# 64 more no-ops a step on TensorE, two behind each W1 product: a step of 768 instruction places

## The chip, the core and the metric

The kernel runs on one core of a Trainium2 chip. A core has five engines with an instruction stream each: TensorE (PE in the profile; its weight loads are shown apart, as PEld), VectorE (DVE), ScalarE (ACT), GpSimd (POOL) and SyncE (SP), which here issues nearly all DMAs. They run side by side and wait for each other through semaphores. The metric is the device time of one launch in microseconds, the median of several executions.

## The reference

A block of a transformer with cross attention, over 128 sequences of 128 tokens, model width 256, 16 heads of 16, hidden width 1024, all in float32:

```python
q = (query @ Wq + bq).reshape(b, s, N_HEADS, D_K).transpose(0, 2, 1, 3)
k = (key @ Wk + bk)...          # v in the same way
scores = jnp.einsum('bhqd,bhkd->bhqk', q, k) / jnp.sqrt(jnp.float32(D_K))
scores = jnp.where(j < i + mask, scores, NEG_INF)      # mask is 0
attn = jax.nn.softmax(scores, axis=-1)                 # row 0 is set to zero
ctx = jnp.einsum('bhqk,bhkd->bhqd', attn, v)
x = layer_norm(query + ctx @ Wo + bo, ln1_g, ln1_b)
ffn = jax.nn.relu(x @ W1 + b1) @ W2 + b2
out = layer_norm(x + ffn, ln2_g, ln2_b)
```

## The kernel before

The sequences are taken in 64 pairs, and the work on a pair is spread over several turns of a software pipeline. `steps(9, 60)` (L1669) emits 52 turns of it, here called steps or slots; slots 7 and 8 and the last ones are written out by hand, op by op, in other orders. The order inside a step is the list `order` in `step_tables` (L1643). It is an order of emission: each engine runs its own instructions of it strictly in that order, and waits where an operand isn't ready. A name in the list with slot p works on pair p for the scores, on older pairs for the later stages: p - 2 for the context and Wo, p - 3 for the hidden layer, p - 4 for the second layer.

TensorE's part of a step, in its order, is this:

- `scores` (`scores_both`, L494, matmuls at L510): 32 float32 products on strips of 32 rows. A float32 product is two weight loads and two matmuls, so the profile counts 64 matmuls.
- the queries of the next pair (`q261`, `q457`, `q3`; L354), the output projection (`out`, `o457`, `o3`; L722), keys (`k`, L284) and values (`v`, L414), with parts of the following mixed in.
- the hidden layer, class `Hidden`, stages H1 to H7 (matmuls at L1282). Seven block products in place of eight; each stage is a loop over NI = 4, so there are 28 W1 products a step. H1 reads `x1T`, the transposed first norm, which comes back from DRAM by DMA (`x1out` and `x1in`, L1004 to L1012); H1 is the first to wait for it.
- the second layer, class `Second`, stages S1 to S7 (L1184), again 28 products. They accumulate in tiles named pX, py and pz.
- `weigh` (L657 and L667): softmax weights times values, 48 small products, whose 96 matmuls stand straight ahead of the scores of the next step. The last stages ahead of it are, in order, H7, S7, H2, H4, H3.

`empty(n)` (L219) emits n no-ops on TensorE, with `nofuse=True` so that they stay instructions of their own. They compute nothing and nothing waits for them. `Second` spreads `pads` of them over its 28 products, through the difference of two rounded quotients, so that 56 are two behind each:

```python
1188                     self.done += 1
1189                     empty(self.pads * self.done // (7 * K) - self.pads * (self.done - 1) // (7 * K))
```

`Hidden` emits none. `second7` (L1472) and `hidden7` (L1475) make the two objects of a slot, once each, for the slots from 7 to 62; the tail makes its own, without pads.

An instruction place is one instruction of TensorE's stream: a weight load, a matmul, a no-op or a semaphore instruction. A step of the loop has the same places each time.

## Time and profile before

| what | us |
|---|---|
| median of 3 runs | 1508.13 |
| lowest, highest | 1504.8, 1508.3 |
| the profiled execution | 1508.24 |
| its span, from first to last instruction | 1506.3 |
| DMA queue q1 (data) | 218.36 MB, 60.7% of 16 engines' time |
| largest group of matmuls, L1282, x1T times w | 128.9 busy, 960 of 277 ns |
| scores, L510 | 108.4 busy by the page's group, 3840 matmuls in 60 steps |

The page's busy times count an engine as busy while it has an instruction in flight. Matmuls overlap, and their ends are modelled, so TensorE's busy share is high even where it could go faster; an idle time printed for it is a lower bound of what it lost. In a row of the timeline stand the start, the length, the engine, the source line, the operation, the tiles written and read, the shape and the count of merged instructions; in square brackets the idle time before it and what ended it. "issue" says that the engine waited for nothing that the profile shows. In the view by stretch of time the columns are the stretch, its length, busy time (with the count) of PE, PEld, DVE, ACT and POOL, TensorE's granted clock, the DMA engines' share and GB/s.

### The profile page before, as it was taken

To read this page: it belongs to the slowest core of one execution; us is meant where nothing else is said; L and a number is where in the kernel's file an instruction comes from. 1 tells how busy PE (TensorE), PEld (TensorE's weight loads), DVE (VectorE), ACT (ScalarE), POOL (GpSimd) and SP (SyncE) were. 2 spreads that over 40 slices of the span, in tenths; PEclk is the share of its full clock that TensorE was granted. 3 is DMA by queue.
4 is the path that set the end of the run, shared out by engine and by line. 5 is a ranking of instruction groups with operands and counts; after the bars stand their busy time and mean duration, and the time that the engine had idled before them with its cause. 6 is when DMAs were issued, how large, how long until landed. Compare 5 with 4: busy or idle time off the path is not lost.

```text
span 1506.3 us, 58023 instructions
## 1 busy us (share of the span) xinstructions
PE 1472.7 (98%) x20054; PEld 1385.7 (92%) x20054; DVE 1314.4 (87%) x2955; ACT 1334.7 (89%) x5336; POOL 1375.2 (91%) x1772
## 2 busy tenths in 40 slices
PE   9999999999999999999999999999999999999998
PEld 6788899999999999999999999999999999999988
DVE  7999789889889898898898888988888988988876
ACT  5658899999999999999999989999999999999963
POOL 7888799999999999899999999999999998999998
PEclk9999999999999999999999999999999999999999
DMA  8546566666666656666566666666666566664461
GB/s 202 109 95 155 132 152 155 150 157 144 165 154 148 155 145 157 161 144 157 140 154 155 160 145 149 157 144 162 150 156 148 138 164 159 145 152 130 127 178 57
DMA packets 433155, 222.34 MB, mean 148 GB/s; under 512 B 290412, under 2 KB 394092, under 8 KB 432876
## 3 DMA queue, kind: packets, MB, share of 16 engines
q1 hardware_dynamic: 431356, 218.36, 60.7%
q8 instruction: 173, 2.83, 0.8%
q14 instruction: 106, 0.87, 0.2%
q10 hardware_dynamic: 1520, 0.27, 0.1%
HBM read 86.78 MB, written 35.80 MB: 81 GB/s over the span
## 4 chain that ended last, share of the span: by engine, by line
PE 90%; DMA 2%; DVE 2%; SPq 2%; issue 2%; POOL 1%; ACT 1%; ACTq 0%; DVEq 0%; POOLq 0%
PE phs L1282 25%; PE pX L1184 10%; PE py L1184 7%; PE pz L1184 7%; PE pk L284 7%; PE pss L510 6%; PE pv L414 6%; PE pq L354 6%; PE po L722 5%; PE pc L667 4%; PE pc L657 2%; DMA x1T<-x1t 2%; PE ph L1034 1%; SPq L623 1%; DVE sm L524 1%
## 5 line engine op out<-in xcount | busy, mean ns | idle before, releaser
L1114 ACT ACTIVATE sm<-pss,nmx 128x128 f32<-128x128 f32 x944 | 329.9, 376 | 6.1 <-DVE nmx L1097 3.9
L1114 ACT ACTIVATE sm<-sm,nmx 128x64 f32<-128x64 f32 x944 | 320.1, 362 | 0.7
L589 DVE STREAM_TRANSPOSE tb<-sm 128x1024 f32<-128x1024 f32 x186 | 225.8, 1216 | 3.3 <-POOL sm L563 3.2
L1319 ACT ACTIVATE hT<-hT,b1e_c 128x256 f32<-128x256 f32 x480 | 209.4, 499 | 8.2 <-DVE hT L1310 6.4
L1114 ACT ACTIVATION_READ_ACCUMULATOR sm<-pss,nmx 128x1 f32 x912 | 196.6, 216 | 0.0
L1114 ACT ACTIVATION_READ_ACCUMULATOR sm<-sm,nmx 128x1 f32 x912 | 195.5, 214 | 0.0
L1097 DVE TENSOR_REDUCE nmx<-pss 128x4 f32<-128x512 f32 x236 | 161.3, 685 | 2.2
L404 ACT ACTIVATE kT<-pk,bkh,half 128x256 f32<-128x256 f32 x252 | 139.0, 579 | 2.8 <-PE pk L284 2.8
L1282 PE MATMUL phs<-x1T,w 128*128 128x128 f32 x960 | 128.9, 277 | 5.3 <-DMA x1T<-x1t 5.2
L1282 PEld LDWEIGHTS phs<-x1T,w 128*128 128x128 f32 x960 | 120.1, 193 | 12.9 <-issue 10.3
L524 DVE TENSOR_TENSOR sm<-pss,neg 128x256 f32<-128x256 f32 (+1 forms) x276 | 114.6, 436 | 18.5 <-PE pss L510 13.2
L1282 PE MATMUL phs<-xS,w 128*128 128x128 f32 x960 | 127.0, 275 | 0.0
L510 PE MATMUL pss<-kT,qT 32*64 32x256 f32 (+1 forms) x3840 | 108.4, 330 | 15.9 <-issue 15.5
L414 PE MATMUL pv<-wv,cT 128*128 128x256 f32 x512 | 121.4, 380 | 0.0
L284 PE MATMUL pk<-cT,wk 128*128 128x256 f32 x504 | 119.4, 380 | 0.1
L1208 DVE TENSOR_TENSOR t<-t,pX 128x128 f32<-128x128 f32 x180 | 59.0, 328 | 67.6 <-PE pX L1184 67.6
L1282 PE MATMUL phs<-xS,w1t 128*128 128x128 f32 x960 | 117.8, 275 | 0.0
L1282 PEld LDWEIGHTS phs<-xS,w 128*128 128x128 f32 x960 | 116.8, 192 | 0.1
L1282 PEld LDWEIGHTS phs<-xS,w1t 128*128 128x128 f32 x960 | 112.6, 192 | 0.1
L510 PEld LDWEIGHTS pss<-kT,qT 32*64 32x64 f32 x3840 | 83.5, 131 | 31.7 <-issue 23.4
L1091 DVE TENSOR_TENSOR pss<-pss,neg 128x256 f32<-128x256 f32 x236 | 100.1, 425 | 10.2 <-PE pss L510 10.1
L414 PEld LDWEIGHTS pv<-wv,cT 128*128 128x128 f32 x512 | 93.0, 191 | 10.8 <-issue 0.6
(231 smaller groups left out, 4735.2 us busy)
## 6 DMA issues: line engine op xcount, KB each, us to landing
pT<-tb SPq DMA_DIRECT2D x976, 96.0 KB
x1t<-tbx SPq DMA_DIRECT2D x252, 64.0 KB
x1T<-x1t SPq DMA_DIRECT2D x63, 256.0 KB
out_dram<-t SPq DMA_DIRECT2D x63, 256.0 KB
xb<-in_x_dram SPq DMA_DIRECT2D x124, 128.0 KB
cb<-in_ctx_dram SPq DMA_DIRECT2D x124, 128.0 KB
x<-in_x_dram SPq DMA_DIRECT2D x31, 512.0 KB
wt<-rtd SPq DMA_DIRECT2D x29, 256.0 KB
```

What stands on the lines that cost most here:

```text
L284: nc.tensor.matmul(ps[:, m * TP : (m + 1) * TP], w[:, k, m * P : (m + 1) * P], src[:, k, :], start=(k == 0), stop=(k == KC - 1),)
L404: nc.scalar.activation(st["kT"][:, m, e, :], pk[:, m * TP : (m + 1) * TP], AF.Identity, bias=bkh[:, m, e : e + 1], scale=half[:, e : e + 1],)
L414: nc.tensor.matmul(pv[:, s * D : (s + 1) * D], st["cT"][:, k, s * P : (s + 1) * P], wv[:, k, :], start=(k == 0), stop=(k == KC - 1),)
L510: nc.tensor.matmul(st["sps", hi][r][s * HP : (s + 1) * HP, m * 2 * n : (m + 1) * 2 * n].rearrange("p (e j) -> p e j", e=2), st["qT"][strip ...
L524: nc.vector.tensor_tensor(probabilities(p, hi)[:, 4 * r : 4 * r + 4, :], st["sps", hi][r][:, : 4 * n].rearrange("p (n j) -> p n j", j=n), ...
L589: nc.vector.transpose(st["tb"][:, :, at : at + 256].rearrange("p j (n a) -> p n j a", a=32), probabilities(p, hi).rearrange("p h j -> p (h ...
L1091: nc.vector.tensor_tensor(ps[:, :, HP:], ps[:, :, HP:], neg[:, 1, None, :].to_broadcast([P, 4, HP]), ALU.add)
L1097: nc.vector.tensor_reduce(maxima(p, 1)[:, 4 * r : 4 * r + 4], st["sps", 1][r].rearrange("p (n j) -> p n j", j=P), AX.X, ALU.max, negate=True,)
L1114: nc.scalar.activation(sm[:, h, :], src, AF.Exp, bias=nmx[:, h : h + 1], scale=1.0, **({"accum_out": su[:, u : u + 1]} if summed else {}))
L1184: nc.tensor.matmul(out, left(k), right(k), start=(first and k == 0), stop=(k == K - 1), skip_group_check=True,)
L1282: nc.tensor.matmul(ps[:, i * P : (i + 1) * P].rearrange("p (n a) -> p n a", a=32), left(i), right, start=(i == 0 and which not in self.ONT ...
L1319: nc.scalar.activation(self.hT[:, f], self.hT[:, f], AF.Relu, bias=b1e_c[:, f : f + 1], scale=1.0,)
```

## The change

Each W1 product gets two no-ops behind it in the slots from 9 on, and four in slots 7 and 8; the second layer's no-ops go from 56 to 64 a step. That is 56 + 8 = 64 more places a step, of which the change's description says that a step then counts 768, and that the first score product is moved to place 153 of 256. No operand, tile, bank or order of the other instructions is changed.

```diff
-        def __init__(self, p, banks=None, onto=None):
+        def __init__(self, p, banks=None, onto=None, pads=0):
             st = states[p]
+            self.pads = pads
             if banks:
...
                     left(i), right, start=(i == 0 and which not in self.ONTO),
                     stop=True, skip_group_check=True,
                 )
+                empty(self.pads)
...
     def second7(p):
-        return once("second", p - 4, lambda: Second(p - 4, 56, (5, 7, 3)))
+        return once("second", p - 4, lambda: Second(p - 4, 64, (5, 7, 3)))
 
     def hidden7(p):
-        return once("hidden", p - 3, lambda: Hidden(p - 3, {1: 2, 2: 7, 5: 6, 4: 5}, {3: 5, 6: 1, 7: 1}))
+        return once("hidden", p - 3, lambda: Hidden(p - 3, {1: 2, 2: 7, 5: 6, 4: 5}, {3: 5, 6: 1, 7: 1}, 4 if p < 9 else 2))
```

## The prediction

> **What bounds the kernel now.** I read the page first, then the table of waits of TensorE, then TensorE's timeline over the steady loop.

> ```profile
> span 1506.3 us, 58023 instructions
> PE 1472.7 (98%) x20054; PEld 1385.7 (92%) x20054; DVE 1314.4 (87%) x2955; ACT 1334.7 (89%) x5336; POOL 1375.2 (91%) x1772
> ...
> PEclk9999999999999999999999999999999999999999
> ...
> q8 instruction: 173, 2.83, 0.8%
> ...
> PE 90%; DMA 2%; DVE 2%; SPq 2%; issue 2%; POOL 1%; ACT 1%; ACTq 0%; DVEq 0%; POOLq 0%
> ```

> TensorE is the bound: busy for 98% of the span, 90% of the chain that ended last, its clock at nine tenths or more in every slice. What is left to gain on it is 33 us of idle time and whatever the modelled ends of matmuls hide. The q8 line matters below: instructions come in 173 packets that hold 2.83 MB, so 16.4 KB each. TensorE has 20054 matmuls, 20054 weight loads, 3180 no-ops and about a thousand semaphore instructions, some 44,270 in all; 2.83 MB over these is 64 bytes each, and a packet is 256 instructions. So q8 carries TensorE's own instructions, in **blocks of 256 places**.

> Who does TensorE wait for?

> ```profile
> PE pss L510 <- issue: 15.5, 21, 1.0
> PE phs L1282 <- DMA x1T<-x1t: 5.2, 6, 3.5
> ```

> Twenty-one waits, in the score products alone, are on nothing that the profile knows ("issue"). The timeline, cut to the scores (64 matmuls a step), shows where they fall:

> ```profile
> 213.59 1.62 PE L510 MATMUL pss<-kT,qT 32*64 32x128 f32 x64
> ...
> 554.50 1.62 PE L510 MATMUL pss<-kT,qT 32*64 32x128 f32 x64
> 576.81 1.62 PE L510 MATMUL pss<-kT,qT 32*64 32x128 f32 x64
> 599.12 1.11 PE L510 MATMUL pss<-kT,qT 32*64 32x128 f32 x28
> 601.16 1.11 PE L510 MATMUL pss<-kT,qT 32*64 32x256 f32 x36 [0.94 <-issue]
> 622.96 1.57 PE L510 MATMUL pss<-kT,qT 32*64 32x128 f32 x60
> 625.49 0.43 PE L510 MATMUL pss<-kT,qT 32*64 32x128 f32 x4 [0.97 <-issue]
> 646.62 1.62 PE L510 MATMUL pss<-kT,qT 32*64 32x128 f32 x64
> 669.63 1.62 PE L510 MATMUL pss<-kT,qT 32*64 32x128 f32 x64
> 692.12 1.11 PE L510 MATMUL pss<-kT,qT 32*64 32x128 f32 x28
> 693.91 1.11 PE L510 MATMUL pss<-kT,qT 32*64 32x256 f32 x36 [0.69 <-issue]
> ...
> 1381.52 1.62 PE L510 MATMUL pss<-kT,qT 32*64 32x128 f32 x64
> ```

> Two scores run through, one breaks behind 28 matmuls, one behind 60, and so on with period four. A matmul and its load are two places, so the breaks stand 56 and 120 places behind the first score product. From the break at 625.49 to that at 693.91 it is three steps less 64 places; were these block starts, three steps less 64 must be a multiple of 256, and with a step near 700 places only 704 fits (2048, eight blocks). The change's 768 less its 64 gives the same 704. **The break is the start of a block that has not arrived.** The second witness is q8 itself: the view of DMA packets, asked for 690.9 to 692.7 us, shows one packet there, and none from 687.5 to 690.9 or from 692.7 to 694:

> ```profile
> q8 instruction: 1, 0.02, 5.7%
> ```

> So the block whose absence ends at 693.91 was in flight at 691 to 692.7, about 1.3 us before its first instruction ran.

> What a break costs, from the view of busy time by stretch, with the two whole steps without one:

> ```profile
> 554.50:576.81 22.31, 22.31 (x324) 21.49 (x317) 20.25 (x48) 21.36 (x89) 21.36 (x29) 1.00 0.66 154
> 576.81:599.12 22.31, 22.31 (x323) 21.49 (x317) 20.36 (x48) 21.35 (x89) 21.35 (x29) 1.00 0.64 158
> 622.96:625.93 2.97, 2.00 (x71) 1.55 (x65) 1.86 (x5) 2.58 (x6) 2.57 (x4) 1.00 0.35 82
> 669.63:671.25 1.62, 1.62 (x71) 1.42 (x65) 1.56 (x5) 1.48 (x4) 1.29 (x3) 1.00 0.49 118
> 692.12:695.00 2.88, 2.19 (x72) 1.47 (x65) 1.63 (x5) 2.58 (x6) 2.47 (x4) 1.00 0.39 93
> ```

> A clean step is 22.31 us, TensorE busy throughout, ACT and POOL (the fourth and fifth columns of busy time) near 21.36: a floor that holds twice running. Broken scores take 2.97 or 2.88 instead of 1.62: 1.35 for a printed wait of 0.97 (0.38 more), 1.26 for 0.69 (0.57 more). With 13 breaks of the first sort and 8 of the second, the 21 cost 15.5 + 13 x 0.38 + 8 x 0.57 = **25 us**. Check: the 51 step starts from 213.59 to 1381.52 lie 1167.9 us apart, 51 x 22.31 is 1137.8, the excess 30.1; so about 5 us belong to something else, mainly to this:

> ```profile
> 656.15 1.13 PE L1282 MATMUL phs<-x1T,w 128*128 128x128 f32 x8 [0.47 <-DMA x1T<-x1t]
> ```

> **The change, part by part.**

> *Where blocks now begin.* Slot 27 (622.96) has a block start 120 places behind its first score product. Slot 9 is 18 steps earlier, 18 x 704 = 49.5 blocks, so there it stands at 120 + 128 = 248, which is also 8 ahead. Slots 7 and 8 gain 28 x 4 + 8 = 120 no-ops each, 240 before slot 9's scores: 248 - 240 = **8 places behind the first score product**. From then on 704 + 64 = 768 is three blocks, and every step has this. The other two starts are 248 ahead of the scores and 264 behind.

> *Do the breaks go?* Ahead of the scores stand, counting back, the weighing of values (96 matmuls, 192 places, 5 semaphores), H3 and H4 (four products of four places and now eight no-ops each), then H2. 248 places back is the last product of H2. Timings from the timeline of a clean approach:

> ```profile
> 665.38 1.06 PE L1282 MATMUL phs<-x1T,w 128*128 128x128 f32 x8
> 666.27 1.06 PE L1282 MATMUL phs<-x1T,w1t 128*128 128x128 f32 x8
> 667.16 1.06 PE L1282 MATMUL phs<-xS,w 128*128 128x128 f32 x8
> 668.15 0.43 PE L657 MATMUL pc<-pT,vd 128*32 128x64 f32 x16
> ```

> H2 starts at 665.38, H4 at 666.27, so TensorE is at that block start at about 666.1 and eight places into the scores at 669.7: 3.6 us. The sequencer is there earlier. How much, the no-ops tell, which it runs itself; the view by source line, from 682 to 684.25, beside the loads of the same products (second fence):

> ```profile
> L221 PEldq NOP  x24: 13/13/13, 682.1 to 684.2; - x24
> ```

> ```profile
> 683.29 0.97 PEld L1184 LDWEIGHTS pz<-w,hT 128*128 128x128 f32 x8
> 684.19 0.97 PEld L1184 LDWEIGHTS py<-w,hS 128*128 128x128 f32 x8
> 685.08 0.97 PEld L1184 LDWEIGHTS pz<-wt,hT 128*128 128x128 f32 x8
> ```

> These 24 no-ops belong to the three products; the first is done 1.3 us and the last 1.8 us before their loads. I take 1.5, so 5.1 us pass between the sequencer's entry into a block and the need for the next. What a block needs is bounded by the broken steps: at 692.12 the previous start is 200 places ahead of the scores, in H3's last product, 1.8 us before them in the clean approach: TensorE is there at 690.3, the sequencer at 688.8, and the next block ran at 693.91, 5.1 us later. At 622.96 it lies 136 ahead, inside the weighing, whose 192 places take 1.48 us and where the sequencer is hardly ahead: about 621.6, and 625.49 is 3.9 later. Need 3.9 to 5.1, given 5.1: no break, or one of a few tenths. I put 0.1 us a step, **+5**, between 0 and 20 (0.4 a step). The block entered 8 places behind has some 9 us until the next start, behind H1; the third likewise.

> *The added no-ops.* Two behind each W1 product, 56, and 8 more behind W2 products (64 over 28, two or three each). Their price on the sequencer lies between the 13 ns of the row and (684.2 - 682.1) / 24 = 88 ns, which includes the product's own places; so 0.8 to 5.6 us a step. A product padded twice takes the sequencer about 0.17 us, TensorE 0.89 / 4 = 0.22. TensorE hides them, **0**, while the sequencer is ahead. Without that cover, each costs up to 0.09. With four no-ops (slots 7 and 8) a product needs up to 0.35 and outruns its cover of 1.5 us: 56 products lose at most 0.13 each, 7 us; much of slot 7 waits for data anyway, so I take **+1.3**.

> *What is late next.* H1's wait for x1T. In steps without a break it costs about 5 us over 29, 0.17 each; broken scores give x1T's round trip slack. With 51 unbroken steps, 51 x 0.17 = 8.7, so **+4**.

> Sum: 1506.3 - 25 + 5 + 1.3 + 4 = 1491.6. The profiled execution took 1508.24, 1.9 above its span, and the median is 1508.13: **1493 us**, 1.0% less. Bounds, as measured: 1508.2 - 25 = 1483 with nothing late, 1478 if x1T's 5 us went too; with the terms at their bad ends (20, 7 and 4) 1514.

> [...]

> **Rivals.**

> *Slower: the break moves to place 8 and stays in every step.* For it: need and time given are within tenths, and one bad placement now repeats 51 times. Against: starts 264 and 8 ahead of the scores (669.63) caused no break. It decides when a block takes more than 5.1 us; at 0.5 us a step the gain is gone (25 over 51 steps). With full breaks of 1.3: 1506.3 - 25 + 66 + 5 = 1552, near 1554 measured. The change's own words put the first score product at place 153 of 256. If that zero were a block's start, a block would begin 103 places behind, inside the broken zone, at the same price; the breaks say 8. Chance 0.09.

> *x1T takes over.* If its wait grows to 0.4 us a step, as at 656.15, 51 x 0.4 = 20 instead of 5: 1506.3 - 25 + 15 + 5 + 1.3 = 1503, measured 1505. For it: no slack from breaks, three blocks a step beside its transfers. Against: two steps at 22.31 in a row. Chance 0.13. POOL or ACT as a bound I see below this: 21.36 of 22.31.

> *Blocks are not the cause,* so the change only adds no-ops: 1508 to 1511. [...] Chance 0.04.

> **How the numbers follow.** The forecast has 0.74 (1480 to 1503). A run of this kernel tells about 0.3% from no change, 1503.6 to 1512.6. Faster: the forecast and two thirds of x1T's case, 0.83. Same: the rest of it and the third case, 0.08. Slower: 0.09. The range 1480 to 1508 takes in the forecast, x1T's case, most of the bad ends and the edge of the third; the broken case is left out.

> **What would show it.** Right: no "issue" wait at L510 in the steady loop, scores of 1.62 us, starts 22.3 to 22.6 apart, 187 or 188 packets on q8 (3696 places more are 14.4 blocks). Wrong: scores that break behind 4 matmuls, or behind 51; waits of H1 for x1T beyond 0.2 us a step; gaps between W1 products of slots 7 and 8 beyond 3 us.

## The result, and the profile after

| | before | changed |
|---|---|---|
| median of 4 runs each, us | 1506.47 | 1484.26 |
| lowest, highest | 1502.4, 1508.3 | 1481.78, 1489.55 |
| profiled execution, its span | 1508.24, 1506.3 | 1481.78, 1479.9 |

The ratio is 0.9861, 95% interval 0.9824 to 0.9898. When the changed kernel ran again beside two experiments it was 1481.89 against 1504.55, ratio 0.9842 [0.9823, 0.9862]. By the two intervals the change gains 1.0 to 1.8%. The forecast was 1493 us (1480 to 1508).

The page of the changed kernel, in the lines that answer to those of before:

```profile
span 1479.9 us, 61719 instructions
PE 1464.0 (99%) x20054; PEld 1383.6 (93%) x20054; DVE 1312.3 (89%) x2955; ACT 1330.3 (90%) x5336; POOL 1374.5 (93%) x1772
...
q8 instruction: 187, 3.06, 0.9%
...
PE 92%; DVE 2%; DMA 2%; SPq 1%; POOL 1%; issue 1%; ACT 1%; DVEq 0%; ACTq 0%; POOLq 0%
...
L510 PE MATMUL pss<-kT,qT 32*64 32x128 f32 (+1 forms) x3840 | 97.4, 330 | 0.3 <-ACT hT L1047 0.3
```

There are 3696 instructions more (61719 against 58023), all no-ops: 54 slots with 56 behind W1 products, two (7 and 8) with 112, and 8 behind W2 products in each of the 56. 14 more packets came over q8, 187 for 173, and 0.23 MB, 3.06 for 2.83: 62 bytes for each added no-op and 264 no-ops for each added packet, near the 64 bytes and 256 places that the prediction reckoned from q8's totals (some 47,970 instructions of TensorE over 187 packets are 256.5); q14, the other instruction queue, stayed at 0.87 MB. So more of TensorE's program came in than before, and yet the kernel is faster. A step of the loop can be counted in the traces: 316 weight loads, 316 matmuls, 16 semaphore instructions and 56 no-ops make 704 before; with 120 no-ops it is 768. The score products (L510) are busy for 97.4 us where it was 108.4, with the same count. The table of TensorE's waits begins like this now; the columns are total, times, longest:

```profile
PE phs L1283 <- DMA x1T<-x1t: 2.5, 5, 0.9
PE warm L1350 <- POOL ident masks.py:199: 1.5, 1, 1.5
```

The row of 21 "issue" waits at the scores is gone, and x1T (L1283 here, one line lower) leads, with less than before. The timeline, cut to the scores, near the places that the prediction showed broken, and at the start and end of the loop:

```profile
164.49 1.62 PE L510 MATMUL pss<-kT,qT 32*64 32x128 f32 x64
190.55 1.62 PE L510 MATMUL pss<-kT,qT 32*64 32x128 f32 x64
212.85 1.62 PE L510 MATMUL pss<-kT,qT 32*64 32x128 f32 x64
...
592.89 1.62 PE L510 MATMUL pss<-kT,qT 32*64 32x128 f32 x64
615.50 1.62 PE L510 MATMUL pss<-kT,qT 32*64 32x128 f32 x64
...
1355.59 1.62 PE L510 MATMUL pss<-kT,qT 32*64 32x128 f32 x64
```

All 64 matmuls stand in one row each time: no scores of the loop are broken any more. The 51 steps from 212.85 to 1355.59 take 1142.7 us, 51 x 22.31 is 1137.8, so 4.9 us of excess are left where it was 30.1.

The kernel before had these two rows at the same place, ahead of those that the prediction shows:

```profile
162.78 2.25 PE L510 MATMUL pss<-kT,qT 32*64 32x128 f32 x64
191.28 1.62 PE L510 MATMUL pss<-kT,qT 32*64 32x128 f32 x64
```

Where the 26.4 us between the two spans came from, by the starts of these scores:

| stretch | before | changed | difference |
|---|---|---|---|
| up to the first scores of the loop | 191.28 | 190.55 | -0.7 |
| the loop's 52 steps | 1190.2 | 1165.0 | -25.2 |
| from there to the end | 124.8 | 124.3 | -0.5 |

### The profile page after: what moved, and what is told of

Read it like the earlier page. It is cut to its first block, busy times and chain, and to the rows that moved or that the text cites. A ratio compares the mean times of both kernels' runs of the same rounds, so it can differ in the third digit from the quotient of the medians.

```text
span 1479.9 us, 61719 instructions
## 1 busy us (share of the span) xinstructions
PE 1464.0 (99%) x20054; PEld 1383.6 (93%) x20054; DVE 1312.3 (89%) x2955; ACT 1330.3 (90%) x5336; POOL 1374.5 (93%) x1772
## 3 DMA queue, kind: packets, MB, share of 16 engines
q8 instruction: 187, 3.06, 0.9%
q10 hardware_dynamic: 1520, 0.27, 0.1%
## 4 chain that ended last, share of the span: by engine, by line
PE 92%; DVE 2%; DMA 2%; SPq 1%; POOL 1%; issue 1%; ACT 1%; DVEq 0%; ACTq 0%; POOLq 0%
PE phs L1283 25%; PE pX L1184 10%; PE py L1184 7%; PE pz L1184 7%; PE pk L284 7%; PE pv L414 7%; PE pss L510 6%; PE pq L354 6%; PE po L722 6%; PE pc L667 4%; PE pc L657 2%; DMA x1T<-x1t 2%; PE ph L1034 1%; PE pq L284 1%; DVE sm L524 1%
## 5 line engine op out<-in xcount | busy, mean ns | idle before, releaser
L1283 PE MATMUL phs<-x1T,w 128*128 128x128 f32 x960 | 129.2, 277 | 2.7 <-DMA x1T<-x1t 2.5
L1283 PEld LDWEIGHTS phs<-x1T,w 128*128 128x128 f32 x960 | 119.3, 192 | 11.4 <-issue 7.8
L1283 PE MATMUL phs<-xS,w 128*128 128x128 f32 x960 | 127.8, 276 | 0.0
L1283 PE MATMUL phs<-xS,w1t 128*128 128x128 f32 x960 | 118.3, 276 | 0.0
L1283 PEld LDWEIGHTS phs<-xS,w 128*128 128x128 f32 x960 | 117.4, 192 | 0.3
L1283 PEld LDWEIGHTS phs<-xS,w1t 128*128 128x128 f32 x960 | 113.0, 192 | 0.1
L284 PEld LDWEIGHTS pk<-cT,wk 128*128 128x128 f32 x504 | 91.5, 190 | 10.4 <-ACT sm L1114 0.3
L510 PE MATMUL pss<-kT,qT 32*64 32x128 f32 (+1 forms) x3840 | 97.4, 330 | 0.3 <-ACT hT L1047 0.3
```

Source lines behind the costliest of these rows:

```text
L284: nc.tensor.matmul(ps[:, m * TP : (m + 1) * TP], w[:, k, m * P : (m + 1) * P], src[:, k, :], start=(k == 0), stop=(k == KC - 1),)
L510: nc.tensor.matmul(st["sps", hi][r][s * HP : (s + 1) * HP, m * 2 * n : (m + 1) * 2 * n].rearrange("p (e j) -> p e j", e=2), st["qT"][strip ...
L1283: nc.tensor.matmul(ps[:, i * P : (i + 1) * P].rearrange("p (n a) -> p n a", a=32), left(i), right, start=(i == 0 and which not in self.ONT ...
```

## The experiments

### e1: block starts 112 places later

```diff
-... {3: 5, 6: 1, 7: 1}, 4 if p < 9 else 2))
+... {3: 5, 6: 1, 7: 1}, 2))
```

> Two no-ops behind each W1 product in slots 7 and 8 too, where the changed kernel has four: the step stays at 768 places, and all that moves is the block start, from 56 places ahead of the first score matmul to 56 places behind it. Blocks (a break is a block of 256 that has not arrived when the sequencer gets to it): every step's scores break behind 28 matmuls, for 0.5 to 1.3 us, as 8 such steps of the kernel before did; 1484 + 51 x 0.6 to 1.3 = 1515 to 1550 us; if only from about 570 us on, as there, 1484 + 34 x 1.2 = 1525. Pacing (the no-ops help by themselves, by slowing the sequencer down, and the place is of no consequence): 1484 within 3 us, scores of 1.62 us.

Measured: 1549.29 us (1542.98 to 1552.98), ratio 1.0294 [1.0258, 1.033]. Rows of its timeline, cut to the scores, and, second fence, of its waits:

```profile
236.72 1.11 PE L510 MATMUL pss<-kT,qT 32*64 32x128 f32 x28
238.76 1.11 PE L510 MATMUL pss<-kT,qT 32*64 32x256 f32 x36 [0.94 <-issue]
260.56 1.10 PE L510 MATMUL pss<-kT,qT 32*64 32x128 f32 x28
262.60 1.11 PE L510 MATMUL pss<-kT,qT 32*64 32x256 f32 x36 [0.94 <-issue]
```

```profile
PE pss L510 <- issue: 41.5, 53, 2.5
```

Every one of the 51 steps breaks, each behind the 28th matmul, which is 56 places. With 112 no-ops *fewer*, all in two slots, the kernel is 65 us slower than the changed one. That is what blocks make of it, and what pacing cannot: the loop's own instructions are the same.

### e2: block starts at the place that the prediction named

```diff
-... Second(p - 4, 64, (5, 7, 3)))
+... Second(p - 4, 56 if p < 8 else 64, (5, 7, 3)))
-... {3: 5, 6: 1, 7: 1}, 4 if p < 9 else 2))
+... {3: 5, 6: 1, 7: 1}, 3 if p < 9 else 2))
```

> Three no-ops in slots 7 and 8, and 8 fewer behind W2 in slot 7: the block start stands 8 places behind the first score matmul, where the prediction had put it. Blocks, by the prediction's reckoning (need 3.9 to 5.1 us, given 5.1): breaks of 0 to 0.4 us behind 4 matmuls, 0.1 a step on average, 1484 + 5 = 1489 us, between 1484 and 1504. Pacing: 1484.

Measured: 1510.26 us (1505.81 to 1514.91), ratio 1.0035 [1.002, 1.005]. Its scores, in four steps that follow each other:

```profile
257.60 0.43 PE L510 MATMUL pss<-kT,qT 32*64 32x128 f32 x4
259.11 1.60 PE L510 MATMUL pss<-kT,qT 32*64 32x128 f32 x60 [1.08 <-issue]
281.41 1.62 PE L510 MATMUL pss<-kT,qT 32*64 32x128 f32 x64
303.72 0.43 PE L510 MATMUL pss<-kT,qT 32*64 32x128 f32 x4
304.68 1.61 PE L510 MATMUL pss<-kT,qT 32*64 32x128 f32 x60 [0.53 <-issue]
326.98 1.62 PE L510 MATMUL pss<-kT,qT 32*64 32x128 f32 x64
```

Four matmuls, so 8 places: this kernel, with 64 no-ops fewer than the change, has the block start where the prediction put it, and the change hasn't. Every second step breaks, 24 in the loop, by 1.34 us in the median from one matmul's start to the next. The gain is gone, and the time lies outside the expected 1484 to 1504.

### e3: block starts 112 places behind the first score product

```diff
-... {3: 5, 6: 1, 7: 1}, 4 if p < 9 else 2))
+... {3: 5, 6: 1, 7: 1}, 1 if p < 9 else 2))
```

> One no-op in slots 7 and 8: the block start stands 112 places behind the first score matmul, near the 120 of the kernel before, where all 13 steps broke by 0.7 to 1.2 us. Blocks: every step breaks behind 56 matmuls, 1.0 to 1.35 us each, 1535 to 1553 us, and 21 or so waits on issue become about 50. Pacing: 1484.

Measured: 1543.04 us (1538.15 to 1543.93), ratio 1.025 [1.0222, 1.0279].

```profile
258.95 1.57 PE L510 MATMUL pss<-kT,qT 32*64 32x128 f32 x56
261.35 0.45 PE L510 MATMUL pss<-kT,qT 32*64 32x128 f32 x8 [0.83 <-issue]
```

All 51 steps break, behind 56 matmuls, the place to the unit again.

### e4: other no-ops, the same block starts

From slot 9 on no no-op stands behind a W1 product; two stand behind each of the 22 products of the queries, keys, values and Wo, and W2 has 76. The first line of the cut below is the queries'; keys, values and Wo have one like it.

```diff
+                empty(2 if 9 < self.p < 64 else 0)
...
-... Second(p - 4, 64, (5, 7, 3)))
+... Second(p - 4, 64 if p < 9 else 76, (5, 7, 3)))
-... {3: 5, 6: 1, 7: 1}, 4 if p < 9 else 2))
+... {3: 5, 6: 1, 7: 1}, 4 if p < 9 else 0))
```

> From slot 9 on the added no-ops stand elsewhere: none behind W1 products, two behind each product of queries, output, keys and values (44), 20 more behind W2; step 768, block start 56 ahead of the scores as in the changed kernel. Blocks: the same as the changed kernel, 1484 within 4 us, no break. Pacing of the W1 products: the gain goes, 1500 or more, with waits on issue back in the scores.

Measured: 1485.53 us (1485.25 to 1485.85), ratio 0.9875 [0.9848, 0.9902]; no score product breaks in its trace. Moving the no-ops inside the step made no difference here; that a step has 768 places and where its blocks begin does. Pacing falls with e1 and e4 together.

### e5: why only every second step broke in e2

In e2 the fetch packet of a broken step started about 1 us ahead of its first score product, that of a clean one about 3 us ahead. The packets, for 4 us ahead of the broken scores (252.5 to 256.5) and, second fence, ahead of the clean ones (276 to 280); the columns are packets, MB and the share of 16 engines' time:

```profile
q1 hardware_dynamic: 3618, 0.84, 100.7%
...
x<-in_x_dram SPq DMA_DIRECT2D x1, 512.0 KB
```

```profile
q1 hardware_dynamic: 1932, 0.24, 39.8%
q8 instruction: 1, 0.02, 1.4%
```

In the first the DMA engines are full (100.7%) and no packet of q8 moves; in the second one does, with q1 at 39.8%. The load in the first is that of the tokens, `load_tokens`, 512 KB every second step. So e5 is e2 with that load issued in the other steps:

```diff
         if p % 2 == 0 and p + 4 < NP:
             load([p + 4, p + 5], "x")
+        if p % 2 == 0 and 11 < p < NP - 3:
+            load_tokens(p // 2)
...
-            if 3 < p < NP - 1:
+            if 3 < p < 11 or p == NP - 3:
                 load_tokens((p + 1) // 2)
```

> As e2_place8 (block start 8 places behind the first score product of every step), but from p = 12 on the 512 KB load of the tokens is issued with the block load of x (even p) in place of that of the context (odd p), one step later. If the block's fetch is late because it stands behind the token load: the breaks change sides, that is they go from 257.6, 303.7, 349.3 and so on to the steps between them (near 281, 327, 373), still 22 to 26 of them of 0.5 to 2 us, and the time stays within 1500 to 1520, ratio 0.995 to 1.01. If it is the context's block load or anything else that goes by the step's parity: the breaks stay in the same steps as in e2, same time. If it takes both loads together: none or few breaks, 1485 to 1492, ratio 0.985 to 0.99. By the pacing theory nothing depends on it.

Measured: 1507.92 us (1501.74 to 1510.73), ratio 0.9993 [0.9975, 1.0012].

```profile
369.04 0.43 PE L510 MATMUL pss<-kT,qT 32*64 32x128 f32 x4
370.28 1.60 PE L510 MATMUL pss<-kT,qT 32*64 32x128 f32 x60 [0.80 <-issue]
392.57 1.62 PE L510 MATMUL pss<-kT,qT 32*64 32x128 f32 x64
414.88 0.43 PE L510 MATMUL pss<-kT,qT 32*64 32x128 f32 x4
416.12 1.60 PE L510 MATMUL pss<-kT,qT 32*64 32x128 f32 x60 [0.80 <-issue]
438.41 1.62 PE L510 MATMUL pss<-kT,qT 32*64 32x128 f32 x64
```

Counted by slots, the breaks of e2 were all in even ones (slot 12 at 257.60, 14 at 303.72); here 22 of the 23 are in odd ones (slot 17 at 369.04, 19 at 414.88), all of those from slot 15 on. The breaks went with the token load: **a block's fetch that meets this load comes about 2 us later** (from slot 15 on, the packet began 1.1 us ahead of the scores with the load and 3.1 without it in the median of e2, 1.2 and 3.2 in e5). That decides at this place; in e1 and e3 every step breaks, with the load or without.

### e6, e7, e8: the places between

The same edit with other numbers of no-ops in slots 7 and 8: 4 and 3, 3 and 2, 5 and 4.

> Slots 7 and 8 get 4 and 3 no-ops behind each W1 product: block starts 28 places ahead of the first score product of every step, inside the weighing, and 284 ahead, inside S7 or H2. By the blocks theory TensorE's sequencer enters at 284 ahead about 7.5 us before the scores and needs the block about 0.3 us before them: 7 us against the at most 6.9 that the late fetches of e2 took: no break, or a few; 1483 to 1492, ratio 0.984 to 0.991. If being inside the small products of the weighing were enough for a break, it would break in each step within the weighing (behind 82 of 96 matmuls): 1530 to 1550. By the pacing theory 1485.

> Slots 7 and 8 get 3 and 2 no-ops behind each W1 product: block starts 28 places behind the first score product, and 228 ahead of it, in H4. The sequencer enters about 4.7 us before the scores; between e1 (200 ahead, a break in every step of 0.5 to 1.65) and e2 (248 ahead, every second step). By the blocks theory: breaks behind 14 matmuls, in every step or nearly so, 0.3 to 2 us, 1515 to 1545, ratio 1.007 to 1.028. By the pacing theory as the change, 1485.

> Slots 7 and 8 get 5 and 4 no-ops behind each W1 product: block starts 84 places ahead of the first score product, inside the weighing, and 340 ahead. By the blocks theory no break in any step, as with the change (56 ahead): 1482 to 1490, ratio 0.983 to 0.989, with up to 3 us more in slots 7 and 8 for the no-ops. If slots 7 and 8 lose as the prediction's bound says (0.09 us a no-op), 56 more no-ops cost 5 us: 1490. By the pacing theory 1485.

Measured: e6 1501.85 (1499.25 to 1504.44), ratio 0.9967 [0.9952, 0.9982]; e7 1538.96 (1538.6 to 1539.97), 1.0209 [1.0194, 1.0224]; e8 1489.92 (1489.26 to 1494.14), 0.9889 [0.9867, 0.9912]. In one table, from the traces: breaks in the scores of the 51 steps (a matmul that starts over 0.3 us behind the one before it), the excess of these steps over 51 x 22.31, and how long TensorE itself is in the block before, that is from the matmul 256 places ahead of the block start to the one at it. This last column is an estimate, good to some 0.2 us, from the starts of the matmuls in an unbroken step of the changed kernel:

| block start from the first score product | kernel | ratio | breaks | excess, us | in the block before, us |
|---|---|---|---|---|---|
| 112 behind | e3 | 1.025 | 51 | 61.4 | 2.3 |
| 56 behind | e1 | 1.0294 | 51 | 70.4 | 2.2 |
| 28 behind | e7 | 1.0209 | 49 | 63.6 | 3.0 |
| 8 behind | e2 | 1.0035 | 24 | 38.2 | 3.5 |
| 8 behind, token load moved | e5 | 0.9993 | 23 | 32.4 | 3.5 |
| 28 ahead | e6 | 0.9967 | 0 | 18.0 | 4.5 |
| 56 ahead | the change | 0.9861, 0.9842 | 0 | 4.9 | 5.3 |
| 56 ahead, other no-ops | e4 | 0.9875 | 0 | 6.6 | - |
| 84 ahead | e8 | 0.9889 | 0 | 11.7 | 6.1 |

In these runs the breaks go by the last column: every step at 2.2 and 2.3 us and nearly every one at 3.0, every second step at 3.5, none in the scores from 4.5 on.

e7 came as expected. e6 and e8 have no breaks in the scores, as expected, but e6 missed its time by 10 us or more. Its waits, and, second fence, those of e8:

```profile
PE phs L1283 <- DMA x1T<-x1t: 8.7, 19, 1.4
PE pc L667 <- issue: 3.8, 1, 3.8
```

```profile
PE phs L1283 <- DMA x1T<-x1t: 7.0, 16, 1.1
```

H1 waits for x1T three times as long as in the changed kernel: the prediction's second rival, in part, at other places. Summed over the 51 steps, H1 started 15.0 us late in e6 and 10.2 in e8, where it was 3.7 in the changed kernel; that is most of each excess. So e8's 1490 us are the loop's, and not, as its expectation had it, the price of no-ops in slots 7 and 8: these two slots took 51.7 us, 51.0 in the changed kernel. (The single wait of 3.8 at the weighing is in the tail, behind the loop.)

### e9, e10, e11: is it x1T?

S5 needs nothing from x1T. Put ahead of H1, it gives x1T 0.9 us more. e9 is e6 with this, e10 is the changed kernel with it, e11 is the changed kernel as it is.

```diff
-            ... ("v", 0), ("H1", 0), ("k11", 0),
-            ("lexp14", 0), ("vd1", 0), ("max3", 0), ("oC2", 0), ("S5", 0), ("add0", 0), ...
+            ... ("v", 0), ("S5", 0), ("H1", 0), ("k11", 0),
+            ("lexp14", 0), ("vd1", 0), ("max3", 0), ("oC2", 0), ("add0", 0), ...
```

> e6 (block starts 28 ahead of the scores) lost 14 us in 47 steps to H1 waiting for x1T (H1 starts 8.9 us behind the scores where it doesn't wait, later in 26 steps). Here S5, whose operands are older, stands ahead of H1 instead of behind it, so H1 is due 0.9 us later and everything behind the two at the same time. If e6's loss is x1T's round trip alone: all but some 2 us of the 14 go, 1486 to 1492, ratio 0.987 to 0.991. If x1T only shows a delay that hits other transfers too, or if S5 or the stages behind H1 are late now: 1498 to 1506, ratio 0.995 to 1.0. By the pacing theory there is nothing to gain at H1: 1500.

> The changed kernel with S5 ahead of H1. Its steps were 4 us over 47 x 22.31, 3.2 of it H1's start being late. If that is x1T: 3 us of it go, 1480 to 1484 beside the changed kernel's time of this call, ratio 0.981 to 0.986. If the stages behind H1 (its sums, the ReLUs) are late by the 0.9 us: 1484 to 1495.

> The changed kernel again, for the comparison with e9 and e10 on the same chip: 1482 to 1488, ratio 0.983 to 0.988, no break, x1T waits of 2 to 6 us.

Measured side by side: e9 1494.57 (1492.12 to 1495.65), ratio 0.9924 [0.9906, 0.9942]; e10 1490.96 (1489.54 to 1493.07), 0.9907 [0.989, 0.9924]; e11 1481.89 (1479.18 to 1484.73), 0.9842 [0.9823, 0.9862], as expected to 0.1 us. The waits of e9 and, second fence, of e10:

```profile
PE pc L667 <- issue: 3.6, 4, 1.3
PE phs L1283 <- DMA x1T<-x1t: 2.1, 3, 1.5
```

```profile
PE phs L1283 <- DMA x1T<-x1t: 1.1, 1, 1.1
```

Summed over the 51 steps, H1 started 15.0 us late in e6 and 1.6 us late in e9, each against its own unhindered start, so x1T was e6's loss. But neither e9 nor e10 reached the time expected if x1T alone was late, since the step itself became longer. Two steps of e10 and one of e11, in the view of busy time by stretch:

```profile
258.14:280.74 22.60, 22.58 (x323) 21.56 (x317) 20.23 (x48) 21.29 (x89) 21.54 (x29) 1.00 0.61 144
280.74:303.23 22.49, 22.49 (x322) 21.56 (x316) 20.21 (x48) 21.30 (x89) 21.32 (x29) 1.00 0.70 166
```

```profile
256.50:278.81 22.31, 22.31 (x324) 21.48 (x316) 20.37 (x48) 21.36 (x89) 21.39 (x29) 1.00 0.66 160
```

22.60 and 22.49 take turns, 0.23 above 22.31 on average, 12 us over 51 steps. Matched product by product, the two traces agree to 0.05 us up to S7, and the 0.2 to 0.3 are lost at the first products of H2: a stage behind H1, as the expectation's second case had it, though which operand is late there wasn't followed up. The order with H1 first stays the better one, and no kernel tried here beats the change. e9 also broke in the weighing in four steps of the loop (the row at L667), by 0.2 to 1.3 us, so the start at 28 ahead was not free of breaks either.

## Why the prediction was right, and where it was wrong

**The bound and its cause: right.** Missing blocks of 256 places were what the scores waited for. In e1, e2, e3 and e7 the break moves to the unit where the count of places puts it: behind 28, 4, 56 and 14 matmuls. In all 175 breaks of these four kernels the first matmul behind the break starts 1.0 to 1.6 us after the end of a packet of q8, 1.4 in the median. The price of a break was right too: 25 us for 21 was predicted, and the loop's excess fell by 25.2.

The number of blocks alone does not make the waits: 187 packets come over q8 in the changed kernel and no block start of its loop shows as a wait at the scores, but in e1, with 187 too, 53 waits of 41.5 us in all do.

**"8 places behind the first score product": wrong, this step failed.** The prediction took the scores at 213.59 for slot 9 and so 622.96 for slot 27. But the slot written by hand ends with the long step up to 191.28, and the loop's regular 22.31 us begin there: 191.28 is slot 9, 213.59 is slot 10 and 622.96 is slot 28. Eighteen steps ahead of slot 28 the start is 248 behind the scores of slot 10, one step earlier it is 64 less, 184. Less 240 for slots 7 and 8 that is -56: the change puts its block start 56 places *ahead* of the scores, into the weighing, the others 200 behind and 312 ahead. e2 shows that place 8 needs 64 no-ops fewer than the change has, which is the 64 places by which one step of 704 shifts the starts. Counting TensorE's records from the first of each trace agrees: the number ahead of a break, divided by 256, leaves 192 in before, e1, e2, e3 and e7 alike, and the number ahead of the changed kernel's first score product leaves 248, which is 56 more. So it stands at place 56 of its block, and not at the 153 of the change's description. That the time came out near was luck: two errors ran against each other, a wrong place and too small a price for it.

**"Need 3.9 to 5.1, given 5.1", 0.1 us a step: wrong size.** At the place for which it was reckoned (e2) it would have been 24 breaks of 1.3 us: 1510, outside the range. The range from 3.9 to 5.1 was read from broken steps without asking what set it. At this place e5 shows one thing that does: whether the fetch meets the token load. Need and given were both counted from the sequencer's entry into the block before; that the need runs from there was the author's estimate and was not shown. The term of +5 was 0 at the place where the change really is, since there all 51 scores hold.

**The no-ops "0 in the loop, +1.3 in slots 7 and 8": right in the loop, a little off before it.** Clean steps stay at 22.31. Slot 7 took 24.93 us where it was 22.77, slot 8 took 26.06 where it was 28.50; with 0.45 less ahead of them that is -0.7 in place of +1.3. The other kernels show slot 7 growing with its no-ops: 22.76 us with one or two behind each W1 product (e3, e1), 22.76 and 23.66 with three (e2, e7), 24.4 to 26.0 with four (the change, e4, e6, e9 to e11), 26.96 with five (e8). These lengths fit no-ops that cost TensorE time from about three on; what covers fewer was not shown. But slot 8 takes up part of it, and the two together took 49.5 to 52.6 us in the four kernels that have the same no-ops in both (the change, e4, e10, e11): a term of 1.3 is lost in that spread.

**"x1T +4": did not come.** Its wait is 2.5 us in 5 places instead of 5.2 in 6, and the loop's excess of 4.9 is what was left of before's 30.1 without breaks. The slack that breaks gave x1T was not needed here; e6 and e8 show that the rival was real 28 places away on either side.

Altogether the span fell by 26.4 where 14.7 were summed. The 11.7 between them are +5, +4, 2.0 up to the loop, and 0.7 in the loop's rest and the tail. **The rivals:** the slower one, a break at place 8 in every step, was named with the right mechanism and a price that was double (every second step breaks); its variant, "a block would begin 103 places behind", is near e3, 1543, for which 1554 was given. That the blocks are not the cause fell with the first run.

## What to carry to other kernels

Where TensorE's trace shows "issue" waits that return with a fixed distance in instructions, count places: here the count told to the unit where the breaks came in four kernels, and no-ops ahead of the loop moved them (e1, 1549 us) or ended them (the change, 1484). Make a step's places a multiple of the block as it was counted here (768, three times 256) so that one placement serves every step, put the start where TensorE has long work in the block before it (here 2.2 to 3.5 us broke the scores; at 4.5 four steps of e9 still broke just ahead of them; 5.3 and 6.1 held), and anchor the count on an observed break of the same kernel, not on a slot number. Then look at the DMA queues: in e2 and e5 the packet began 1.1 to 1.2 us ahead of the scores in the steps with the token load and 3.1 to 3.2 in those without.

## What the runs showed that was not expected

In two slots ahead of the loop, 112 no-ops decide over 4% of the whole kernel: e1 and the change have the same loop, and take 1549 and 1484 us.

The packets of q8 seem to hold up SyncE as well, though no run tried that alone. The four DMA issues of x1's way out begin 0.9 us ahead of the scores, and take either some 1.8 us or 2.5 to 3.6: the longer time in 31 of 51 steps of the changed kernel and in 43 of e8. Over the loops of all thirteen traces, in the steps in which a packet of q8 began 0.8 to 1.4 us after the first of these issues, 277 of 279 took over 2.4 us; where none began until 1.9 us after it, none of 75 did. A row of each sort, of SyncE's timeline (start, length), first of e8, then of the changed kernel:

```profile
257.96 3.04 SPq L256 DMA_DIRECT2D x1t<-tbx  x4
```

```profile
323.57 1.79 SPq L256 DMA_DIRECT2D x1t<-tbx  x4
```

Call an issue held if it took over 0.6 us, where a free one takes 0.3 to 0.5. In e8 the third issue was held in 28 steps, in which H1 started 0.27 us late on average; with the fourth held, as mostly in the changed kernel, it was 0.16, with none 0.02. In e6 the 16 steps with no held issue were the later ones, 0.62 us against 0.15 with the fourth held: what makes x1T late there stays open.

In the kernel before, starts 56 places behind the scores held up to slot 23 (508.76), and broke from slot 27 (599.12) on; in e1 they broke from the first step. Ahead of 508.76 the packet began 2.6 us before the scores, ahead of 599.12 only 0.5 us, though TensorE's sequencer was at the same point in both: a semaphore instruction two places behind the earlier block start is recorded 2.96 us ahead of the scores each time. What held the packet back wasn't found, so a placement that holds for some steps need not hold for all.
